# Values of nine tiles moved behind the routed loop, recurrence pieces inside the listing of rows, and gathered rows normalized on ScalarE

## The chip, the cores and the metric

The kernel runs on one core of a Trainium2 chip. A core has five engines that run side by side, each with its own in-order queue of instructions: PE (TensorE, matrix products and transposes), DVE (VectorE), ACT (ScalarE), POOL (GpSimd) and SP (SyncE, which here only issues DMA transfers). They meet through semaphores: an instruction waits until those it needs have signalled. The metric is the device time of one execution in microseconds (us), as the median of several runs; lower is better.

## The reference

There are 2048 tokens of 512 numbers in float32, and two layers. In each the input is normalized per row (`xn`), two branches are computed from `xn`, and `x = x + s * silu(ffn)`.

```python
xn = _layernorm(x)
# layer 0: s is a recurrence over the tokens, per channel
xk, xv, xr = (xn * tm + shifted(xn) * (1 - tm) for tm in (tm_k, tm_v, tm_r))
k, v, r = xk @ Wk.T, xv @ Wv.T, sigmoid(xr @ Wr.T)
def step((aa, bb, pp), (kt, vt)):
    qt = maximum(pp, kt + u); e1 = exp(pp - qt); e2 = exp(kt + u - qt)
    out = (e1 * aa + e2 * vt) / (e1 * bb + e2)
    pn = maximum(pp + neg_ew, kt); f1 = exp(pp - pn); f2 = exp(kt - pn)
    return (f1 * aa + f2 * vt, f1 * bb + f2, pn), out
s = (r * layernorm(out)) @ Wo.T
# layer 0: ffn is the better of 2 experts for each token (512 -> 2048 -> 512)
h = silu(x @ w_gate[e].T) * (x @ w_up[e].T);  y = (h @ w_down[e].T) * top_w
# layer 1: s is attention, keys before the last 256 of a batch averaged in blocks of 64
s = (softmax(mask(q @ k.T)) @ v) @ Wo
# layer 1: ffn is 2 shared experts and the best 4 of 16 routed ones (512 -> 352 -> 512)
rout = sum over the 4 chosen e of g[t, e] * (relu(x @ w1[e] + b1[e]) @ w2[e] + b2[e])
```

## The kernel before, in words

A tile is 128 tokens; there are 16. Python generators hand out pieces of one stage that are put between the matmuls of another, and a scheduler places each engine's instructions from there; `keep_in_program_order` pins an instruction to the place where it was written. PE carries the order of the whole: where it has nothing, other engines are late.

**First stage (lines 177 to 262).** Rows are loaded, normalized on ScalarE (L234), a difference of the two experts' logits `dl` is taken (L238), and each of the 16 tiles is transposed on PE (`transposed`, L139, with a copy on ScalarE, L140) and stored to `xnt0` in HBM (L245). After all 16 stores SP issues the loads of `wv` and `wr` (L248, L249). L250 copies the rows' means into `facts`.

**The listing (L252 to L361).** It lists the rows of each expert, so that tiles of 128 rows belong to one expert: `sel` (L253) on VectorE, sums with PE (`tab`, L271), a chain of small VectorE operations for the place of each row, then `put` (three operations, L343) and four `hot` matrices (L350), and 32 matmuls (L355) that bring row number, mean and `rstd` to their places. `tok` (L359) and `row_mr` (L360) are copies of the result. 17 tiles of listed rows come out, in pairs: nine steps of the expert loop, one of them a single tile.

**The recurrence (L386 to L536).** `recurrence(b)` handles a block of 256 tokens; 8 blocks of 22 pieces. A block loads `xT0` from `xnt0` (L393, L395), carries the last state over on ScalarE (L397), takes `diff` on GpSimd (L400), three mixes `xm` of four VectorE operations each (L406), projections on PE (L416) with copies of k and v on ScalarE (L428, L452), scans on VectorE (L435, L478), `f1`, `f2`, `qt` on VectorE (L459 to L463), `e1`, `e2` on GpSimd (L464, L465), two sigmoids and two Exps on ScalarE (L467 to L471), and the products, GpSimd taking `v` (L484), `den` (L492) and `r` (L534). Before the expert loop the generator is advanced by seven pieces (L692); the rest is spread over the loop.

**The expert loop of layer 0.** `rows0` gathers the listed rows on GpSimd's DMA queue (L545, four buffers `xr`), normalizes them on VectorE (L552), transposes them (`tp`, L560) and copies the result on ScalarE (`xg`, L563). `up0` makes `pg` on PE (L571, three PSUM buffers), `sg` on ScalarE (L576), `hT` on VectorE (L578). `down0` (L593) runs two steps behind. Each pair has 16 such steps. SP loads the weights in eight parts per pair (L157, L161), four buffers.

**The routed loop of layer 1 (L1715).** 80 tiles are laid out, of which those that hold rows run (later ones in a conditional). A tile has `tp` (L1661), `xg` (L1663), `ph` (L1668), `ht` (L943), `py` (L1692), `y` (L1697) and a scatter-add into `comb` on GpSimd's queue (L1700). Weights come on SP (L659 to L662). Pieces of the attention are put between the tiles: per block the queries and the scores, and for tiles 0 to 7 (`WIDE` is 8) the values. `PARTS` (L1706) is their number, 40. Tiles 0 to 7 have few pooled keys ("near", `vo8`), tiles 8 to 13 more ("wide", `vo`). `values` transposes the probabilities (`pt`, L1590), copies them on ScalarE (`sT`, L1595), multiplies with V and Wo already joined (`pw`, L1600) and copies to `xT` (L1604).

**The tail (L1737 to L1773).** Sums are loaded from `comb` (L1744) once all scatters have landed. `values` of tiles 8 to 11 follow, then `close(0)`, `close(2)`, `values(12)`, `close(4)`, `close(6)`, `values(13)` and the last four. A `close` handles two tiles: Silu on ScalarE (L1752, pinned), a product with `xT` (L1754) and a sum (L1758) on VectorE, and the store (L1759).

Of the kernel before, what the change touches and what calls it, by code (L numbers as in the profile page):

```python
# [17 lines left out]
P = 128  # L18
T = 2048
D = 512  # L20
# [57 lines left out]
def tile_kernel(ctx: ExitStack, tc: tile.TileContext, a: dict):  # L78
# [89 lines left out]


# [55 lines left out]
    for i in range(0, NT, 2):  # L225
        xin = xins[i // 2]
        mv, rstd = norm_stats(xin, 2, all_mv[:, i : i + 2, :], facts[:, 2, i : i + 2])
        shift = small.tile([P, 2], F32, tag="shift", name="shift")
# [3 lines left out]
        for j in range(2):  # L232
            xn = xin[:, j, :]
            nc.scalar.activation(  # L234
                xn, xn, AF.Identity, bias=shift[:, j : j + 1], scale=rstd[:, j : j + 1],
            )
            junk = n0.tile([P, D], F32, tag="hot", bufs=2, name="junk")
            nc.vector.tensor_tensor_reduce(  # L238
                out=junk, in0=xn, in1=wdiff, scale=1.0, scalar=0.0, op0=ALU.mult, op1=ALU.add,
                accum_out=dl[:, i + j : i + j + 1],  # L240
            )
    for i in range(NT):
        xt = n0.tile([P, NC, P], F32, tag="xt", name="xt")
        transposed(n0ps, xins[i // 2][:, i % 2, :], xt, "tp")
        nc.sync.dma_start(out=xnt0[:, :, i * P : (i + 1) * P], in_=xt)  # L245
    wv = rc.tile([P, NC, D], F32, name="wv")
    wr = rc.tile([P, NC, D], F32, name="wr")
    tc.keep_in_program_order(nc.sync.dma_start(out=wv, in_=a["Wv"]))  # L248
    tc.keep_in_program_order(nc.sync.dma_start(out=wr, in_=a["Wr"]))  # L249
    nc.vector.tensor_copy(facts[:, 1, :], all_mv[:, :, 0])  # L250

    sel = n0.tile([P, NT, E0], F32, bufs=1, name="sel")  # L252
    nc.vector.tensor_scalar(  # L253
        out=sel[:, :, 0], in0=dl, scalar1=0.0, scalar2=None, op0=ALU.is_le
    )
    nc.vector.tensor_scalar(
# [83 lines left out]

    put = n0.tile([P, NT, 3, NST], F32, bufs=1, name="put")
# [6 lines left out]
    for i0 in range(0, NT, HN):  # L348
        hot = n0.tile([P, HN, P], F32, tag="hot", bufs=2, name="hot")
# [20 lines left out]
    zero = rc.tile([P, DX], F32, name="zero")  # L370
    nc.gpsimd.memset(zero, 0.0)
    S4 = [P, NC, RB]
    ones = rc.tile([P, P], F32, name="ones")
    nc.vector.memset(ones, 1.0 / D)
    nge = rc.tile([P, NC], F32, name="nge")
    nc.scalar.activation(nge, vecs[:, VEC.index("decay"), :], AF.Exp)
    nc.vector.tensor_scalar(out=nge, in0=nge, scalar1=-1.0, scalar2=None, op0=ALU.mult)

    st_p = rc.tile([P, NC, RB + 1], F32, name="st_p")
    st_a = rc.tile([P, NC, RB + 1], F32, name="st_a")  # L380
    st_b = rc.tile([P, NC, RB + 1], F32, name="st_b")
    nc.vector.memset(st_p[:, :, 0:1], -1.0e38)
    nc.vector.memset(st_a[:, :, 0:1], 0.0)
    nc.vector.memset(st_b[:, :, 0:1], 0.0)

    def recurrence(b):  # L386

        t0 = b * RB

        xT0 = rb.tile([P, NC, RB + 1], F32, tag="xT0", bufs=2, name="xT0")  # L390
        if b == 0:
            nc.vector.memset(xT0[:, :, 0:1], 0.0)
            nc.sync.dma_start(out=xT0[:, :, 1:], in_=xnt0[:, :, 0:RB])  # L393
        else:
            nc.sync.dma_start(out=xT0, in_=xnt0[:, :, t0 - 1 : t0 + RB])  # L395
            for st in (st_p, st_a, st_b):
                nc.scalar.copy(st[:, :, 0:1], st[:, :, RB : RB + 1])  # L397
        cur, prev = xT0[:, :, 1 : 1 + RB], xT0[:, :, 0:RB]
        diff = rb.tile(S4, F32, tag="diff", name="diff")
        nc.gpsimd.tensor_tensor(out=diff, in0=cur, in1=prev, op=ALU.subtract)  # L400
        yield

        def mixed(tm):
            xm = rb.tile(S4, F32, tag="xm", bufs=3, name="xm")
            for c in range(NC):
                nc.vector.scalar_tensor_tensor(  # L406
                    out=xm[:, c, :], in0=diff[:, c, :], scalar=vec(tm, c),
                    in1=prev[:, c, :], op0=ALU.mult, op1=ALU.add,
                )
            return xm  # L410

        def project(xm, w_, o0):
            ps = rps.tile([P, 2, RB], F32, tag="proj", name="proj")
            for j in range(2):
                for c in range(NC):
                    nc.tensor.matmul(  # L416
                        out=ps[:, j, :], lhsT=w_[:, c, (o0 + j) * P : (o0 + j + 1) * P],
                        rhs=xm[:, c, :], start=(c == 0), stop=(c == NC - 1),
                    )
            return ps  # L420

        k = rb.tile(S4, F32, tag="k", name="k")
        ku = rb.tile(S4, F32, tag="ku", name="ku")
        v = rb.tile(S4, F32, tag="v", name="v")
        r = rb.tile(S4, F32, tag="r", name="r")

        def take_k(o0, ps):
            nc.scalar.copy(k[:, o0 : o0 + 2, :], ps)  # L428
            for j in range(2):
                nc.scalar.activation(  # L430
                    ku[:, o0 + j, :], ps[:, j, :], AF.Identity, bias=vec("first", o0 + j)
                )

        def scan_p(c):
            nc.vector.tensor_tensor_scan(  # L435
                out=st_p[:, c, 1 : RB + 1],
                data0=nge[:, c : c + 1].to_broadcast([P, RB]),
                data1=k[:, c, :], initial=st_p[:, c, 0:1], op0=ALU.add, op1=ALU.max,
            )

        xk = mixed("tm_k")
        yield
        xv = mixed("tm_v")
        take_k(0, project(xk, wk, 0))
        yield
        xr = mixed("tm_r")
        take_k(2, project(xk, wk, 2))
        yield
        for o0 in (0, 2):
            scan_p(o0)  # L450
            scan_p(o0 + 1)
            nc.scalar.copy(v[:, o0 : o0 + 2, :], project(xv, wv, o0))  # L452
            yield
        pp, ppn = st_p[:, :, 0:RB], st_p[:, :, 1 : RB + 1]
        ex = rb.tile([P, 4, NC, RB], F32, tag="ex", name="ex")
        e1, e2, f1, f2 = (ex[:, i] for i in range(4))
        qt = rb.tile(S4, F32, tag="qt", name="qt")
        r01 = project(xr, wr, 0)
        nc.vector.tensor_tensor(out=f1, in0=pp, in1=ppn, op=ALU.subtract)  # L459
        nc.vector.tensor_tensor(out=f2, in0=k, in1=ppn, op=ALU.subtract)  # L460
        yield
        r23 = project(xr, wr, 2)
        nc.vector.tensor_tensor(out=qt, in0=pp, in1=ku, op=ALU.max)  # L463
        nc.gpsimd.tensor_tensor(out=e1, in0=pp, in1=qt, op=ALU.subtract)  # L464
        nc.gpsimd.tensor_tensor(out=e2, in0=ku, in1=qt, op=ALU.subtract)  # L465
        yield
        nc.scalar.activation(r[:, 0:2, :], r01, AF.Sigmoid)  # L467
        nc.scalar.activation(r[:, 2:4, :], r23, AF.Sigmoid)
        yield
        nc.scalar.activation(ex[:, 2:4], ex[:, 2:4], AF.Exp)  # L470
        nc.scalar.activation(ex[:, 0:2], ex[:, 0:2], AF.Exp)  # L471
        fv = qt
        nc.vector.tensor_tensor(out=fv, in0=f2, in1=v, op=ALU.mult)
        yield

        def scan(st, add, cs):
            for c in cs:
                nc.vector.tensor_tensor_scan(  # L478
                    out=st[:, c, 1 : RB + 1], data0=f1[:, c, :], data1=add[:, c, :],
                    initial=st[:, c, 0:1], op0=ALU.mult, op1=ALU.add,  # L480
                )

        scan(st_a, fv, (0, 1))
        nc.gpsimd.tensor_tensor(out=v, in0=e2, in1=v, op=ALU.mult)  # L484
        yield
        scan(st_a, fv, (2, 3))
        yield
        scan(st_b, f2, range(NC))
        yield
        num, den = ku, fv  # L490
        nc.vector.tensor_tensor(out=num, in0=e1, in1=st_a[:, :, 0:RB], op=ALU.mult)
        nc.gpsimd.tensor_tensor(out=den, in0=e1, in1=st_b[:, :, 0:RB], op=ALU.mult)  # L492
        yield
        nc.vector.tensor_tensor(out=num, in0=num, in1=v, op=ALU.add)
        nc.vector.tensor_tensor(out=den, in0=den, in1=e2, op=ALU.add)
        yield
        for c0 in (0, 2):
            for c in (c0, c0 + 1):
                nc.vector.reciprocal(out=den[:, c, :], in_=den[:, c, :])
            yield  # L500


        two = rb.tile([P, 2, RB], F32, tag="two", name="two")

        def mean(src):

            nc.vector.tensor_tensor(out=two, in0=src[:, 0:2], in1=src[:, 2:4], op=ALU.add)
            nc.vector.tensor_tensor(
                out=two[:, 0, :], in0=two[:, 0, :], in1=two[:, 1, :], op=ALU.add
            )  # L510
            pm = f0t.tile([P, 2, RB], F32, tag="tp", name="pm")[:, 0, :]
# [1254 lines left out]
    for i in (0, 2):  # L1766
        close(i)
# [100 lines left out]
```

## Time and profile before

| | us |
|---|---|
| runs: lowest, median, highest of 3 | 1935.80, 1936.94, 1939.53 |
| the profiled execution | 1930.89 |
| its span on the core | 1929.2 |
| PE busy in the span | 1849.7 |
| mean granted PE clock | 0.984 of full |
| first expert matmul `pg` starts | 81.48 |
| last matmul of the routed loop ends | 1878.64 |
| first product of the tail on VectorE starts | 1900.49 |

The span runs from the first to the last instruction on the core; 1.69 us of the profiled execution lie around it. A row of a timeline gives the start, the busy time, the engine, the source line, the operation, the output and inputs with their shapes, how many instructions were joined, and in brackets the idle time before it on its engine with what ended it. PEld is PE's loading of weights; a letter q behind an engine's name means its queue of other instructions. A row of windows gives for a stretch the busy time and number of instructions of PE, PEld, DVE, ACT and POOL, then the granted clock, the busy share of the DMA engines and the GB/s. A row of waits gives who waited for whom: total, times, longest.

### The profile page before, as it was taken

What the parts mean: (1) busy time and instruction counts of PE and PEld (TensorE: products, weight loads), DVE (VectorE), ACT (ScalarE), POOL (GpSimd) and SP (SyncE); (2) the same over time, 40 slices, a digit from 0 to 9 for tenths busy, and PEclk for the clock granted to TensorE, in tenths of its full rate; (3) what the DMA queues carried; (4) which work ended last, traced back from release to release, by engine and by line L of the source; (5) the groups of instructions that cost most, each with busy time, mean ns of one, the idle gap of its engine ahead of it and who ended that gap; (6) DMA issues with size and microseconds to landing.
All of it is one profiled execution on the core that took longest, in us unless ns stands there. A gap on an engine that the chain in (4) does not pass through costs nothing. (4 is left out here: it accounts for less than half of the span.)

```text
span 1929.2 us, 23186 instructions
## 1 busy us (share of the span) xinstructions
PE 1849.7 (96%) x8107; PEld 1286.6 (67%) x8107; DVE 772.0 (40%) x1544; ACT 525.4 (27%) x989; POOL 467.0 (24%) x351
## 2 busy tenths in 40 slices
PE   5899999999999999999999999999999999999994
PEld 4677777787877777777533654445777777777662
DVE  8713637272634545252175543421323323233313
ACT  6213222232323232232134212221222222222222
POOL 1301212120201111020210453000344444444340
PEclk8899999999999999999999999999999999999997
DMA  7657685635654443536461553122999999999895
GB/s 252 208 156 265 222 304 180 216 106 165 197 192 142 132 131 124 160 97 229 155 227 48 177 206 115 50 82 83 316 291 311 325 283 277 276 269 269 232 254 183
DMA packets 214096, 381.35 MB, mean 198 GB/s; under 512 B 16972, under 2 KB 134476, under 8 KB 213080
## 3 DMA queue, kind: packets, MB, share of 16 engines
q1 hardware_dynamic: 183896, 332.78, 51.5%
q0 software_dynamic: 28784, 45.63, 10.8%
q10 hardware_dynamic: 1296, 1.41, 0.3%
q8 instruction: 67, 1.10, 0.2%
q14 instruction: 53, 0.43, 0.1%
HBM read 294.04 MB, written 85.72 MB: 197 GB/s over the span
## 5 line engine op out<-in xcount | busy, mean ns | idle before, releaser
L571 PE MATMUL pg<-xg,w 128*128 128x256 f32 (+1 forms) x2304 | 495.0, 367 | 3.6 <-ACT xg L563 3.6
L571 PEld LDWEIGHTS pg<-xg,w 128*128 128x128 f32 x2304 | 419.0, 190 | 94.4 <-issue 42.1
L1700 POOL DMA_INDIRECT comb<-y,to x146 | 227.5, 1558 | 317.6 <-DMA comb<-y,to 210.4
L593 PE MATMUL py<-wd,hT 128*128 128x512 f32 x544 | 256.9, 593 | 2.9 <-DVE hT L578 2.9
L1668 PEld LDWEIGHTS ph<-xg,w 128*128 128x128 f32 (+1 forms) x1776 | 201.9, 182 | 38.3 <-ACT xg L1663 33.3
L1668 PE MATMUL ph<-xg,w 128*128 128x128 f32 (+1 forms) x1776 | 214.5, 277 | 1.2 <-DMA w<-in_w_dram 1.2
L1692 PE MATMUL py<-w,ht 128*128 128x512 f32 (+1 forms) x438 | 207.8, 593 | 0.0
L578 DVE TENSOR_TENSOR hT<-sg,pg 128x256 f32<-128x256 f32 (+1 forms) x144 | 57.1, 402 | 335.7 <-ACT sg L576 335.6
L576 ACT ACTIVATE sg<-pg 128x256 f32<-128x256 f32 (+1 forms) x144 | 53.5, 372 | 416.9 <-PE pg L571 416.6
L593 PEld LDWEIGHTS py<-wd,hT 128*128 128x128 f32 x544 | 102.1, 190 | 72.2 <-issue 61.9
L1697 DVE TENSOR_SCALAR y<-py,g 128x512 f32<-128x512 f32 x73 | 54.6, 749 | 228.1 <-PE py L1692 228.1
L943 ACT ACTIVATE ht<-ph,b1t 128x128 f32<-128x128 f32 (+1 forms) x222 | 81.3, 366 | 178.5 <-PE ph L1668 178.0
L1692 PEld LDWEIGHTS py<-w,ht 128*128 128x128 f32 (+1 forms) x438 | 76.2, 191 | 53.3 <-issue 51.9
L1663 ACT COPY xg<-tp 128x512 f32<-128x512 f32 x74 | 43.4, 586 | 188.0 <-PE tp L1661 188.0
L1106 PE MATMUL py<-w,hT 128*128 128x512 f32 (+1 forms) x192 | 89.4, 595 | 0.0
L957 PE MATMUL ph<-xT,w 128*128 128x512 f32 (+1 forms) x192 | 88.0, 597 | 0.0
L1044 POOL DMA_INDIRECT xs<-acc,slot x64 | 64.0, 1000 | 65.9 <-DMA xs<-acc,slot 44.5
L416 PE MATMUL proj<-xm,wr 128*128 128x256 f32 x256 | 60.7, 392 | 5.8 <-ACT v L452 5.8
L712 PE MATMUL po<-wo,yb 128*128 128x512 f32 x128 | 58.9, 620 | 6.5 <-ACT acc L721 6.5
L464 POOL TENSOR_TENSOR ex<-st_p,qt 128x1024 f32<-128x1024 f32 x8 | 18.3, 2288 | 192.8 <-DVE qt L463 192.8
L1661 PEld LDWEIGHTS tp<-ident,x 128*128 128x128 f32 x296 | 36.7, 140 | 38.8 <-issue 20.8
L545 POOL DMA_INDIRECT xr<-in_x_dram,tok x17 | 23.2, 1365 | 160.4 <-PE tp L560 133.2
(412 smaller groups left out, 2182.7 us busy)
## 6 DMA issues: line engine op xcount, KB each, us to landing
w<-in_w_dram SPq DMA_DIRECT2D x76, 704.0 KB
w<-in_w_dram SPq DMA_DIRECT2D x76, 512.0 KB
w<-in_w_gate_dram SPq DMA_DIRECT2D x72, 512.0 KB
w<-in_w_up_dram SPq DMA_DIRECT2D x72, 512.0 KB
wd<-in_w_down_dram SPq DMA_DIRECT2D x72, 512.0 KB
xs<-zero SPq DMA_DIRECT2D x16, 1360.0 KB
x<-xs SPq DMA_DIRECT2D x74, 272.0 KB
w<-in_w_dram SPq DMA_DIRECT2D x76, 192.0 KB
```

The source lines that it names most:

```text
L416: nc.tensor.matmul(out=ps[:, j, :], lhsT=w_[:, c, (o0 + j) * P : (o0 + j + 1) * P], rhs=xm[:, c, :], start=(c == 0), stop=(c == NC - 1),)
L571: nc.tensor.matmul(out=pg[:, i, 0:n], lhsT=w[:, c, i * FH + f * P : i * FH + (f + 1) * P], rhs=xg[:, c, 0:n], start=(c == 0), stop=(c == N ...
L578: nc.vector.tensor_tensor(out=hT[:, 0:n], in0=sg[:, 0:n], in1=pg[:, 1, 0:n], op=ALU.mult)
L593: nc.tensor.matmul(out=p, lhsT=hT[:, u * P : (u + 1) * P], rhs=wd[:, f, :], start=first_, stop=last_,)
L712: nc.tensor.matmul(out=po, lhsT=yb[:, c, s * P : (s + 1) * P], rhs=wo[:, c, :], start=(c == 0), stop=(c == NC - 1),)
L943: nc.scalar.activation(dst, src, AF.Relu, bias=b)
L957: nc.tensor.matmul(out=ph[0:n, :], lhsT=up(w, f, n, c), rhs=xT[:, c, cols], start=(c == 0), stop=(c == NC - 1),)
L1044: ins = nc.gpsimd.indirect_dma_start(out=xs, out_offset=bass.IndirectOffsetOnAxis(ap=slot[:, i, k : k + 1], axis=0), in_=acc[:, i, :], in_ ...
L1106: nc.tensor.matmul(out=py, lhsT=hT[0:n, e, f, s * P : (s + 1) * P], rhs=down(w, f, n), start=(e == 0 and f == 0), stop=(e == NS - 1 and f ...
L1668: nc.tensor.matmul(out=ph[0:n, :], lhsT=up(w, f, n, c), rhs=xg[:, c, :], start=(c == 0), stop=(c == NC - 1),)
L1692: nc.tensor.matmul(out=py, lhsT=hT[0:n, f, :], rhs=down(w, f, n), start=(f == 0), stop=(f == NF1 - 1),)
L1700: nc.gpsimd.indirect_dma_start(out=c_, out_offset=bass.IndirectOffsetOnAxis(ap=to, axis=0), in_=y[:, h * D // 2 : (h + 1) * D // 2], in_of ...
```

## The change

1. `zero`, `ones`, `nge`, the states and `recurrence` are defined before the first stage. Two pieces are issued before `sel`, one before `put`, one before the third `hot`, and two more before the expert loop (six ahead of it; seven before). `diff` of blocks 0 and 1 goes to VectorE. Block 0's Exps, block 1's copies of the states and the first operation of `sel` are pinned.
2. `wv` and `wr` are loaded at tiles 4 and 8 of the transposes.
3. `shift` (minus mean times `rstd`) is written into `facts` in place of the mean, and gathered rows are normalized as `x * rstd + shift` on ScalarE.
4. `values` is cut in two: `turned` (transposes and the `sT` copy) and `values` (the matmuls and the `xT` copy). Tiles 5 to 13 (`LAST`) have theirs behind the routed loop, each tile's `turned` issued before the `values` of the tile ahead of it; `turned` of these takes PSUM from the pool of `py`. `PARTS` is 37. `close(0)` and `close(2)` follow the values of tile 11, 4 and 6 those of 12, 8 and 10 those of 13, then 14 and 12.

`recurrence` is the same code but for the lines shown.

```diff
+    zero = rc.tile([P, DX], F32, name="zero")
...
+    def recurrence(b):
...
             for st in (st_p, st_a, st_b):
-                nc.scalar.copy(st[:, :, 0:1], st[:, :, RB : RB + 1])
+                ins = nc.scalar.copy(st[:, :, 0:1], st[:, :, RB : RB + 1])
+                if b == 1:
+                    tc.keep_in_program_order(ins)
...
-        nc.gpsimd.tensor_tensor(out=diff, in0=cur, in1=prev, op=ALU.subtract)
+        (nc.vector if b < 2 else nc.gpsimd).tensor_tensor(
+            out=diff, in0=cur, in1=prev, op=ALU.subtract
+        )
...
-        nc.scalar.activation(ex[:, 2:4], ex[:, 2:4], AF.Exp)
-        nc.scalar.activation(ex[:, 0:2], ex[:, 0:2], AF.Exp)
+        ins = nc.scalar.activation(ex[:, 2:4], ex[:, 2:4], AF.Exp)
+        if b == 0:
+            tc.keep_in_program_order(ins)
+        ins = nc.scalar.activation(ex[:, 0:2], ex[:, 0:2], AF.Exp)
+        if b == 0:
+            tc.keep_in_program_order(ins)
...
-        shift = small.tile([P, 2], F32, tag="shift", name="shift")
+        shift = facts[:, 1, i : i + 2]
...
+    wv = rc.tile([P, NC, D], F32, name="wv")
+    wr = rc.tile([P, NC, D], F32, name="wr")
     for i in range(NT):
         xt = n0.tile([P, NC, P], F32, tag="xt", name="xt")
         transposed(n0ps, xins[i // 2][:, i % 2, :], xt, "tp")
         nc.sync.dma_start(out=xnt0[:, :, i * P : (i + 1) * P], in_=xt)
-    wv = rc.tile([P, NC, D], F32, name="wv")
-    wr = rc.tile([P, NC, D], F32, name="wr")
-    tc.keep_in_program_order(nc.sync.dma_start(out=wv, in_=a["Wv"]))
-    tc.keep_in_program_order(nc.sync.dma_start(out=wr, in_=a["Wr"]))
-    nc.vector.tensor_copy(facts[:, 1, :], all_mv[:, :, 0])
-
+        for at, w_, nm in ((4, wv, "Wv"), (8, wr, "Wr")):
+            if i == at:
+                tc.keep_in_program_order(nc.sync.dma_start(out=w_, in_=a[nm]))
+
+    blocks = (piece for b in range(NRB) for piece in recurrence(b))
+    for _ in range(2):
+        next(blocks)
...
+    tc.keep_in_program_order(ins)
...
+    next(blocks)
     put = n0.tile([P, NT, 3, NST], F32, bufs=1, name="put")
...
     for i0 in range(0, NT, HN):
+        if i0 == 2 * HN:
+            next(blocks)
         hot = n0.tile([P, HN, P], F32, tag="hot", bufs=2, name="hot")
...
-            nc.vector.tensor_scalar(
-                out=xr, in0=xr, scalar1=row_mr[:, 0, j : j + 1],
-                scalar2=row_mr[:, 1, j : j + 1], op0=ALU.subtract, op1=ALU.mult,
-            )
+            nc.scalar.activation(
+                xr, xr, AF.Identity, bias=row_mr[:, 0, j : j + 1], scale=row_mr[:, 1, j : j + 1]
+            )
...
-    for _ in range(7):
+    for _ in range(6 - done):
         next(blocks)
         done += 1
...
-    def values(i, s, pinned=False):
+    def turned(i):
+
+        s = waiting.pop(i)
         keys = s.shape[2]
         each = P // keys
-        by_row = vo if keys == KP else vo8
         nw = H // each
-        pt = aps.tile([P, nw, P], F32, tag="pa", name="pt")
+
+        pool, tag = (m1y, "py") if i in LAST else (aps, "pa")
+        pt = pool.tile([P, nw, P], F32, tag=tag, name="pt")
...
         sT = aq2.tile([P, HKV, P], F32, tag="sT", name="sT")
-        ins = nc.scalar.copy(sT[:, 0:nw, :], pt)
-        if pinned:
-            tc.keep_in_program_order(ins)
+        nc.scalar.copy(sT[:, 0:nw, :], pt)
+        return i, nw, sT, vo if keys == KP else vo8
+
+    def values(i, nw, sT, by_row):
...
+    LAST = range(5, FULL[0])
...
-                if i < WIDE:
-                    values(i, waiting.pop(i))
+                if i not in LAST:
+                    values(*turned(i))
                     yield
...
-    PARTS = 4 * nb + WIDE
+    PARTS = 4 * nb + LAST[0]
...
-    for i in (8, 9, 10, 11):
-        values(i, waiting.pop(i), pinned=True)
-    for i in (0, 2):
-        close(i)
-    values(12, waiting.pop(12), pinned=True)
-    for i in (4, 6):
-        close(i)
-    values(13, waiting.pop(13), pinned=True)
-    for i in (8, 10, 14, 12):
-        close(i)
+
+    pinned = tc.keep_in_program_order
+    closing = [i for i in range(0, NT, 2) if i < LAST[0] - 1]
+    closing += [i for i in (*range(0, NT, 2),) if i not in closing and i != FULL[0] - 2]
+    closing += [FULL[0] - 2]
+    ahead = turned(LAST[0])
+    for i in LAST:
+        now, ahead = ahead, turned(i + 1) if i + 1 in LAST else None
+        values(*now)
+        if i >= LAST[-1] - 2:
+            for _ in range(2):
+                close(closing.pop(0))
+    for i in closing:
+        close(i)
```

## The prediction

> **What bounds the kernel now.** I read the page's busy shares and slices first, then the timeline of the first 82 us and of the last 55, then the waits and the windows between.
>
> ```profile
> PE 1849.7 (96%) x8107; PEld 1286.6 (67%) x8107; DVE 772.0 (40%) x1544; ACT 525.4 (27%) x989; POOL 467.0 (24%) x351
> ...
> PE   5899999999999999999999999999999999999994
> ...
> PEclk8899999999999999999999999999999999999997
> ```
>
> TensorE works 96% of the span, at a lower clock only in the first two slices and the last. So only two things can move the end: matmul time taken off PE, and PE's holes, which sit at both ends. The windows and waits say it of the routed loop:
>
> ```profile
> 560.00:910.00 350.00, 350.00 (x1418) 267.00 (x1417) 148.25 (x184) 100.55 (x156) 47.05 (x21) 1.00 0.44 141
> 1400.00:1876.00 476.00, 475.30 (x2656) 344.39 (x2656) 136.50 (x442) 121.84 (x288) 203.01 (x132) 1.00 0.97 281
> ```
>
> ```profile
> SPq L660 <- PE py L1692: 196.3, 58, 7.2
> ```
>
> In the loop PE is busy 475.3 of 476 us, and the weight queue (L660) waits 196.3 us for PE's buffers: PE bounds it, though the DMA share is 0.97. The start, by its timeline:
>
> ```profile
> 37.22 2.33 POOL L400 TENSOR_TENSOR diff<-xT 128x1024 f32<-128x1024 f32 x1 [9.47 <-DVE run L279]
> ...
> 37.77 1.80 DVE L288 TENSOR_TENSOR full<-run,eno 128x8 f32<-128x8 f32 x1
> ...
> 46.54 7.07 PE L355 MATMUL tab<-put,hot 128*128 128x51 f32 x32 [5.31 <-DVE put L343]
> ...
> 53.64 0.18 DVE L359 CAST tok<-tab 128x17 int32<-128x17 f32 x1 [1.42 <-PE tab L355]
> ...
> 67.61 6.41 PE L416 MATMUL proj<-xm,wr 128*128 128x256 f32 x16 [5.77 <-ACT v L452]
> ...
> 81.48 0.70 PE L571 MATMUL pg<-xg,w 128*128 128x256 f32 x2 [3.56 <-ACT xg L563]
> ```
>
> Three holes of 5.31, 5.77 and 3.56 us. The first waits for the listing; the second for a ScalarE copy of v, queued behind an Exp that waits for GpSimd's e2 (62.79 to 65.14); the third for the copy of the gathered rows, queued behind state copies that wait for GpSimd. The first expert matmul starts at 81.48. The tail:
>
> ```profile
> 1881.22 0.63 PE L1590 MATMUL pt<-ident,wide 128*128 128x128 f32 x4 [2.91 <-PEq L1717]
> ...
> 1892.74 9.44 SPq L1744 DMA_DIRECT2D y<-comb  x16
> ...
> 1900.49 2.36 DVE L1754 TENSOR_TENSOR y<-xT,y 128x1024 f32<-128x1024 f32 x2 [24.18 <-DMA y<-comb]
> 1901.31 0.57 ACT L1595 COPY sT<-pt 128x512 f32<-128x512 f32 x1
> 1901.93 0.30 PEld L1600 LDWEIGHTS pw<-vo,sT 128*128 128x128 f32 x2 [4.26 <-ACT sT L1595]
> 1901.93 5.40 PE L1600 MATMUL pw<-vo,sT 128*128 128x512 f32 x8 [4.03 <-ACT sT L1595]
> ...
> 1908.94 2.36 DVE L1754 TENSOR_TENSOR y<-xT,y 128x1024 f32<-128x1024 f32 x2 [3.81 <-ACT y L1752]
> ```
>
> The loop's last matmul ends at 1878.64 (call it L). From 1900.49 VectorE sets the end: 16 operations at a pitch of 1.15 = 18.4 us, two holes (3.81, 2.12), then 4.33 us for the last store: the span's end is L+50.56.
>
> **The change, part by part.**
>
> *Tail.* Values of tiles 5, 6, 7 (1.79 us each: a loop tile's period is 7.61 with one, 5.82 without) and of tile 8 (1821.04 to 1825.85 with its pw, 4.81) leave the loop: 3 x 1.79 + 4.81 = 10.18 us of PE. In the tail PE now does 5 to 11 before the first Silu: 3 x 1.79 + 4 x 4.30 (0.60 + 3.70) = 22.6 (the 0.7 that each pw waited for its sT copy is covered by the next tile's transposes), plus 1.5 for the cold clock (pw took 5.20 after the 2.91 hole, 3.70 warm): from L+2.91 to L+27.0. Then the xT copy 0.59, the Silu's table load 1.28, half a pair of Silus 1.06: VectorE starts at L+29.9. The loads of comb (issued after a wait for the last scatter, landed L+19 before) are no longer last, and no longer on the path. Because tiles 12 and 13 are turned ahead, pw 12 ends by L+31.3 and pw 13 by L+35.1, Silus 4 and 6 by L+33.8: VectorE runs its 16 operations without a hole, 18.4, then 4.33: L+52.6. That is 2.0 later against L, with L 10.2 earlier: **-8.1**. Bounds: -9.6 if the clock stays up through the first hole, -6.5 if one more pair of VectorE operations waits (1.6).
>
> The trace has pw at 3.70 us after the hole of 2.61 (1910.38) and at 5.40 after 4.03. [...]
>
> *Start, listing.* VectorE gets more to do between sel (L253) and tok (L359): f1, f2 and qt of block 0 (L459 to L463, 1.13 pitch, 3.4 us; before they stood behind tok), diff of block 1 (1.22), and the last scans and mixes. GpSimd's e1 and e2 (2.19 + 2.35) then start right behind qt, near 47.4, and end near 51.9, in the middle of the listing, where VectorE's next operations are mixes with two SBUF inputs. An operation of 128x8 took 1.80 us beside GpSimd's diff (rows above), ending 0.02 after it; of a mix beside GpSimd no row exists. Between 0.48 (unhindered) and a wait to the end of e2 I take the latter, the nearest row: 4.2 us. So put ends near 55.1 (before 46.5: +3.4 +4.2 +1.0 for the other pieces, net of the 0.9 that sel is earlier), the tab matmuls take 7.07 plus two cold projections of 0.93, tok comes at 64.0, **10 us later than before**, and the gathers start at 65.1.
>
> [...]
>
> *Start, after the listing.* What waited behind the gathers is gone from the path: v copies stand ahead on ScalarE, e1 and e2 end before the gathers, both block-0 Exps stand after the first seven sg (L576). By the view of their line, gathers landed 3.3 to 7.6 us after issue (median 6.5), the slow ones under a DMA share of 1.02 at 346 GB/s (41 to 69 us). wv and wr are loaded earlier (at transposes 4 and 8; SP's loads of xnt0 and of FFN weights stand behind them, 4 weight buffers fill by about 62), so I take 4: 69. Normalization on ScalarE 0.75, tp 0.60, copy 0.58, the second tile's 0.75 + 0.60 + 0.58 and a sigmoid 0.60 between them; PE fills with 9 projections of wr until 70.5. First pg at 69 + 0.75 + 0.60 + 0.58 + 0.60 + 0.75 + 0.60 + 0.58 = 73.5, and I add 0.8 for queues: **74.3, or 7.2 earlier**. Bounds: 3.9 earlier if the landing takes 7.3, 11.4 if GpSimd blocks nothing. Besides, five projection matmuls more are done before the first pg: 5 x 0.464 = **-2.3**.
>
> *Normalization on ScalarE* (L552, 17 tiles). VectorE waited 42.4 us for gathers, 8.2 at most; now ScalarE's queue waits and the next sg stands behind. At 143.66 a gather was issued and landed by 151.33: 7.7, of which ScalarE would stand 5 to 6. The cover is three PSUM buffers of pg and down0 two steps behind, some two steps of 5.17 = 10 us; the first pair is nearest to it, as rows 5 and 6 (gathers after the first transposes) hold the first sg until about 83.5, with PE covered to 84.5. I take 0; bounds 0 to +2. Without that cover each of 8 pairs would cost 2 to 5.
>
> *The rest.* The copy of means (L250, 1.73 under GpSimd's diff) goes, and both diffs of 1.9 and 2.33 on GpSimd become 1.22 on VectorE; that makes sel 0.9 earlier and is in the walk. The pinned Exps wait for e2, done 25 us before they are reached; the pinned state copies stand among sg and wait for scans done by then; behind both is only sg, under the same cover of 10 us. On SP the loads of blocks 2 and 3 (L395) stand behind the first four weight sets, and the fifth set behind block 3's, which waits for VectorE's last mix of block 1: four steps, 20 us, cover it. Block 0's recurrence ends later, with PE at 350.00 of 350 us up to 910, so none of it is at the end. The loop's attention pieces go from 40 to 37 over the same 73 tiles: 0.
>
> **Sum**: -8.1 - 7.2 - 2.3 + 0 = -17.6. The profiled execution took 1930.89 (span 1929.2 and 1.69 around it), giving 1913.3; the median shown is 6.05 above it, so 1936.94 - 17.6 = **1919.3**. Bounds together: -11.4 - 2.3 - 9.6 = -23.3, and -3.9 - 2.3 - 6.5 + 2 = -10.7.
>
> **Rivals.** A. *The start gives nothing*: listing 10 later, landing slow, PE finds no work: first pg at 81.5 with the projections lost in the hole. For it: tok's delay is sure. Against: the removed waits (5.77 + 3.56 and cold clocks). Only the tail: 1936.94 - 8.1 = 1928.8.
>
> B. *The loop is set by DMA*: share 0.97, POOL waits 210.4 us for scatters. Then the loop keeps its length, the tail grows by 2.0: -9.5 + 2.0 = -7.5, 1929.4. Against: PE 475.3 of 476, and 346 GB/s moved elsewhere against 281.
>
> C. *ScalarE's queue behind late gathers*, the slower side. Place: sg behind the normalization in FFN. For it: rows that waited 8.2; single-tile steps are only 2.6 us (a hole of 2.9 at 529 to 546). It decides from a hold of about 10 us, and the sum turns slower once 8 pairs lose over 2.7 each (17.6 + 3.9 over 8); at 3 each, +6.4: 1943.
>
> D. *A and B together*: only the tail's 2.0 is left, 1938.9: within the bound of 0.2% (3.9 us, what can be told from no change).
>
> **How the numbers follow.** Forecast 0.60 (1919.3; 1913.6 to 1926.2), A 0.14, B 0.10, D 0.06, C 0.10. Faster 0.84, same 0.06, slower 0.10. The range goes from the lower bound, 1913, to just past A and B, 1931; outside are C, D and some of the forecast's ends.
>
> **What would show it.** Right: tok near 64, e1/e2 near 47 to 52 with a long VectorE row beside them, first pg near 74, the loop's last matmul 19.7 earlier (7.2 + 2.3 + 10.2), VectorE's last 16 operations without holes from about L+30. Wrong: first pg after 80; PE holes at 0.5 us and more ending in hT or sg during the FFN; loop periods unchanged where values left; y<-comb still the last wait of the tail.

## The result and the profile after

The changed kernel takes **1918.81 us** (median of 6 runs, 1917.98 to 1922.52) against 1936.38 us (median of 6, 1934.57 to 1939.53): ratio 0.9911, 95% interval 0.9898 to 0.9924, faster by 17.6 us. The profiled execution took 1917.98, its span is 1916.3. The forecast was 1919.3.

The page of the changed kernel: busy shares, PE and its clock in 40 slices.

```profile
PE 1846.6 (96%) x8107; PEld 1286.1 (67%) x8107; DVE 761.6 (40%) x1528; ACT 536.3 (28%) x1006; POOL 460.9 (24%) x349
...
PE   5999999999999999999999999999999999999996
...
PEclk9899999999999999999999999999999999999998
```

PE is still 96% busy; 3.1 us of its work are gone (1849.7 to 1846.6) and the span is 12.9 shorter, so most of the gain is holes. The windows inside the expert loop and the routed loop, and the weight queue's waits:

```profile
545.00:935.00 390.00, 389.96 (x1576) 296.80 (x1575) 148.98 (x189) 105.27 (x166) 47.04 (x21) 1.00 0.45 146
1385.00:1860.00 475.00, 474.82 (x2682) 346.15 (x2682) 139.35 (x457) 120.91 (x287) 201.71 (x130) 1.00 0.98 286
```

```profile
SPq L674 <- PE py L1710: 204.0, 59, 8.5
```

PE is busy 474.82 of 475 us in the routed loop and the weight queue still waits for PE's buffers, 204.0 us: taking 10 us of PE out has not made the DMA the bound, at a share of 0.98. The start, by its timeline:

```profile
48.18 2.17 POOL L267 TENSOR_TENSOR ex<-st_p,qt 128x1024 f32<-128x1024 f32 x1 [44.88 <-DVE qt L266]
48.35 2.28 DVE L209 SCALAR_TENSOR_TENSOR xm<-diff,vecs,xT 128x256 f32<-128x256 f32 x1
...
50.31 2.53 POOL L268 TENSOR_TENSOR ex<-ku,qt 128x1024 f32<-128x1024 f32 x1
...
50.56 2.32 DVE L512 TENSOR_SCALAR at<-at 128x16 f32<-128x16 f32 x1
...
55.41 3.66 PE L538 MATMUL tab<-put,hot 128*128 128x51 f32 x16 [3.00 <-DVE put L524]
...
64.22 0.18 DVE L542 CAST tok<-tab 128x17 int32<-128x17 f32 x1 [3.63 <-PE tab L538]
...
65.44 1.20 POOL L560 DMA_INDIRECT xr<-in_x_dram,tok  x1 [12.61 <-DMA w<-in_w_up_dram]
...
70.45 1.52 ACT L567 ACTIVATE xr<-xr,row_mr 128x512 f32<-128x512 f32 x2 [3.80 <-DMA xr<-in_x_dram,tok]
...
74.45 7.72 PE L585 MATMUL pg<-xg,w 128*128 128x256 f32 x35
...
81.12 0.82 ACT L590 ACTIVATE sg<-pg 128x256 f32<-128x256 f32 x2
```

e1 and e2 (L267, L268) stand in the listing. A mix (L209) takes 2.28 and a 128x16 operation (L512) 2.32, and they end 0.28 and 0.04 after GpSimd's. tok comes at 64.22, 10.6 later than before; the first rows have landed at 70.45, and the first pg starts at 74.45, 7.0 earlier. The tail:

```profile
1859.51 2.92 PE L1686 MATMUL ph<-xg,w 128*128 128x128 f32 x24
...
1866.80 0.69 PE L1606 MATMUL pt<-ident,near 128*128 128x128 f32 x4 [4.37 <-PEq L1735]
...
1882.36 9.89 SPq L1762 DMA_DIRECT2D y<-comb  x16
...
1890.74 0.58 ACT L1621 COPY xT<-pw 128x512 f32<-128x512 f32 x1 [2.79 <-PE pw L1617]
...
1891.34 1.28 ACT L1770 ACT_TABLE_LOAD   x1
...
1892.63 2.00 ACT L1770 ACTIVATE y<-y 128x1024 f32<-128x1024 f32 x2
...
1893.72 2.36 DVE L1772 TENSOR_TENSOR y<-xT,y 128x1024 f32<-128x1024 f32 x2 [33.29 <-ACT y L1770]
...
1895.16 3.70 PE L1617 MATMUL pw<-vo,sT 128*128 128x512 f32 x8 [0.59 <-ACT sT L1611]
...
1909.62 2.36 DVE L1776 TENSOR_TENSOR y<-y,xo 128x1024 f32<-128x1024 f32 x2
```

The loop's last matmul ends at 1859.51 + 2.92 = 1862.43 (L; before, by the same rows, 1878.31: the 1878.64 given further up is 0.33 too late, which moves no difference here). VectorE starts at L+31.3, 1.1 us after the first Silu starts, and runs to the end without a hole. The span ends at L+53.9. ScalarE goes from the xT copy of tile 11 to the table load and the Silu without a hole, so VectorE's start is set by PE's matmuls and these operations, not by the sums from comb. (The other six executions of this tail show the same on ScalarE, though the profile puts VectorE's wait there down to y<-comb: the label names the signal that came last by the profile.) The row of the kernel before with "24.18 <-DMA y<-comb" has to be read in the same way, for there, too, ScalarE had no hole:

```profile
1897.51 0.59 ACT L1604 COPY xT<-pw 128x512 f32<-128x512 f32 x1 [3.79 <-PE pw L1600]
1898.11 1.28 ACT L1752 ACT_TABLE_LOAD   x1
1899.40 2.00 ACT L1752 ACTIVATE y<-y 128x1024 f32<-128x1024 f32 x2
```

Only in its second profile (before_again) did ScalarE wait for the sums, 0.96 us ahead of the table load and 0.44 ahead of the second Silu.

Stage by stage, in us, for every execution with a profile in this study. "to routed" runs from the last pg to the routed loop's first transpose, "loop" from there to the last ph, "tail" from there to the end; "records" are the projection matmuls before the first pg.

| execution | first pg | records | expert loop | to routed | loop | tail | span |
|---|---|---|---|---|---|---|---|
| before | 81.48 | 94 | 861.9 | 399.8 | 535.1 | 50.8 | 1929.2 |
| before_again | 80.59 | 94 | 863.4 | 401.6 | 534.0 | 52.3 | 1931.9 |
| after | 74.45 | 104 | 860.7 | 399.3 | 528.1 | 53.8 | 1916.3 |
| after_again | 74.93 | 104 | 861.2 | 402.7 | 524.3 | 54.4 | 1917.6 |
| start_alone | 73.48 | 104 | 861.4 | 401.9 | 535.5 | 56.4 | 1928.8 |
| tail_alone | 83.94 | 94 | 865.0 | 402.1 | 526.4 | 54.0 | 1931.4 |
| norm_on_vector | 75.12 | 102 | 861.1 | 401.1 | 524.7 | 53.8 | 1915.7 |
| e1_e2_on_vector | 73.42 | 114 | 858.3 | 403.0 | 528.8 | 55.8 | 1919.3 |
| wv_wr_late | 74.41 | 72 | 869.0 | 404.0 | 524.7 | 53.3 | 1925.3 |
| closes_earlier | 74.50 | 104 | 861.2 | 403.1 | 526.2 | 51.5 | 1916.5 |
| values_5_to_7_in_loop | 74.12 | 104 | 861.1 | 403.1 | 530.0 | 48.7 | 1917.1 |
| both_8 | 75.54 | 114 | 858.7 | 403.8 | 530.5 | 52.8 | 1921.2 |
| both_7_earlier | 73.88 | 114 | 859.0 | 402.2 | 527.7 | 51.1 | 1913.8 |
| rows_before_weights | 70.45 | 114 | 858.8 | 401.7 | 524.0 | 54.2 | 1909.2 |

The stretch "to routed", which no kernel here changes, lies between 399.3 and 404.0: a single profile is good to some 2 us there, and the same in the loop, where the first tile may wait for its weights (below). The old start puts its first pg at 80.6 to 83.9 in three executions.

### The profile page after: what moved, and what is told of

The parts are those of the page before. It is cut to its first block, busy times and chain, and to the rows that moved or that the text cites. A ratio compares the mean times of both kernels' runs of the same rounds, so it can differ in the third digit from the quotient of the medians.

```text
span 1916.3 us, 23192 instructions
## 1 busy us (share of the span) xinstructions
PE 1846.6 (96%) x8107; PEld 1286.1 (67%) x8107; DVE 761.6 (40%) x1528; ACT 536.3 (28%) x1006; POOL 460.9 (24%) x349
## 3 DMA queue, kind: packets, MB, share of 16 engines
q10 hardware_dynamic: 1296, 1.41, 0.2%
## 5 line engine op out<-in xcount | busy, mean ns | idle before, releaser
L267 POOL TENSOR_TENSOR ex<-st_p,qt 128x1024 f32<-128x1024 f32 x8 | 18.3, 2287 | 236.1 <-DVE qt L266 236.1
L219 PE MATMUL proj<-xm,wk 128*128 128x256 f32 x256 | 59.0, 383 | 0.0
```

The costliest lines, as they stand in the source:

```text
L219: nc.tensor.matmul(out=ps[:, j, :], lhsT=w_[:, c, (o0 + j) * P : (o0 + j + 1) * P], rhs=xm[:, c, :], start=(c == 0), stop=(c == NC - 1),)
```

## The experiments

Ratios are to runs of the kernel before on the same chip.

**The two parts by themselves.** `start_alone` is the changed kernel without the hunks on `values`, `LAST`, `PARTS` and the closes; `tail_alone` is the kernel before with these alone.

> The changed kernel with the tail's part undone: recurrence pieces in the listing, early loads of wv and wr, normalization on ScalarE, and the tail as before. My theory: -7.2 for the first expert matmul and -2.3 for projections already done, -9.5 us, ratio near 0.9951; first pg at 74.3. Rival (the gain at the start is lost again later in the expert loop, since ScalarE is held by gathers): ratio 0.998 or more with the first pg still at 74. If the two parts are independent, the two ratios' distances from 1 add up to 0.0089.

> The kernel before with the tail's part alone (values of tiles 5 to 13 behind the routed loop, the next tile turned ahead, new order of the closes). My theory: -8.1 us, a ratio near 0.9958; the routed loop about 9.8 shorter between its first and last matmul, VectorE's last 16 operations without a hole. Rival (the DMA or the scatters set the loop): the loop keeps its length and the run is 0 to 2 us slower, ratio 1.000 to 1.001. Rival (the tail gives nothing, all came from the start): ratio 1.000.

Measured: start_alone 0.9961 (0.9944 to 0.9977), first pg at 73.48; tail_alone 0.9941 (0.9922 to 0.9960), the loop at 526.4 against 534.0 and 535.1. The distances from 1 add up to 0.0098 against 0.0089 for both, as two independent gains would within these intervals: about 8 us for the start and 11 for the tail by the ratios, 7.6 and 9.0 by the medians of the same runs. The rivals in which one part or the loop gives nothing are out. The size of the tail's gain is less sure: in the trace of tail_alone, loop and tail together take 580.4 against 585.9 and 586.3, 5.5 to 5.9 less. The tail of start_alone is the old one, and shows by its timeline what its holes can cost:

```profile
1876.95 0.73 PE L1603 MATMUL pt<-ident,wide 128*128 128x128 f32 x4 [4.60 <-PEq L1730]
...
1878.36 6.57 PE L1613 MATMUL pw<-vo,sT 128*128 128x512 f32 x8 [0.68 <-ACT sT L1608]
...
1899.13 6.42 PE L1613 MATMUL pw<-vo,sT 128*128 128x512 f32 x8 [4.03 <-ACT sT L1608]
...
1908.60 5.11 PE L1613 MATMUL pw<-vo,sT 128*128 128x512 f32 x8 [2.62 <-ACT sT L1608]
```

pw takes 6.57, 6.42 and 5.11 here, after holes of 0.68 (behind one of 4.60), 4.03 and 2.62; in the first profile of before it took 5.20, 5.40 and 3.70, with the last two holes the same (4.03, 2.61). The granted clock over these three pw was 0.71, 0.68 and 1.00 there; by their lengths against the 3.70 at 1.00 it is about 0.56, 0.58 and 0.72 here, an estimate. The old tail thus took 50.8, 52.3 and 56.4 in three executions. Of the 5.6 between the first and the last, 1.7 are the hole behind the loop (4.60 for 2.91) and 3.8 the longer pw (1.37, 1.02 and 1.41); the 52.3 holds the 1.4 us that ScalarE waited for the sums. The new tail has a single long hole and took 53.3 to 55.8 in the seven executions that have it unaltered.

**The normalization's place.**

```diff
-            nc.scalar.activation(
-                xr, xr, AF.Identity, bias=row_mr[:, 0, j : j + 1], scale=row_mr[:, 1, j : j + 1]
-            )
+            nc.vector.tensor_scalar(
+                out=xr, in0=xr, scalar1=row_mr[:, 1, j : j + 1],
+                scalar2=row_mr[:, 0, j : j + 1], op0=ALU.mult, op1=ALU.add,
+            )
```

> The changed kernel with the gathered rows normalized on VectorE again (multiply and add, same order of everything else as far as the scheduler keeps it). My theory: the normalization's place costs or gains nothing in the expert loop, so the ratio to the kernel before stays at 0.991 within 0.001. Rival A (ScalarE held by gathers costs up to 2 us in the changed kernel): 0.990. Rival B (the move is what made the start short, because VectorE is full of mixes there and its rows would be late): first pg later than 76 and a ratio of 0.992 to 0.994.

Measured: 0.9898 (0.9873 to 0.9922), first pg at 75.12, the expert loop 861.1 against 860.7 and 861.2. The ratio by itself does not part the theory (0.991) from rival A (0.990); the expert loop does, as the 2 us of rival A are not in it. No difference: this part of the change costs and gains nothing that can be seen, though ScalarE waits 50.9 us for gathers in the changed kernel, 9.1 at most.

**What GpSimd's e1 and e2 cost the listing.**

```diff
-        nc.gpsimd.tensor_tensor(out=e1, in0=pp, in1=qt, op=ALU.subtract)
-        nc.gpsimd.tensor_tensor(out=e2, in0=ku, in1=qt, op=ALU.subtract)
+        eng = nc.vector if b == 0 else nc.gpsimd
+        eng.tensor_tensor(out=e1, in0=pp, in1=qt, op=ALU.subtract)
+        eng.tensor_tensor(out=e2, in0=ku, in1=qt, op=ALU.subtract)
```

> The changed kernel with e1 and e2 of block 0 on VectorE. If GpSimd's e1 and e2 block VectorE in the listing (mixes of 2.28 and a tensor_scalar of 2.32 in the changed kernel's timeline in place of 0.48 and 0.17, 3.95 us), the block is gone and two operations at 1.13 are added: tok 1.7 us earlier, 62.5 in place of 64.2, and the first pg by 0.8 to 1.7. Rival (the long rows of VectorE had another cause): the long rows stay and tok is 2.3 us later, 66.5.

Its timeline, the same operations as above:

```profile
48.51 1.22 DVE L268 TENSOR_TENSOR ex<-st_p,qt 128x1024 f32<-128x1024 f32 x1
...
49.64 0.17 DVE L513 TENSOR_SCALAR at<-at 128x16 f32<-128x16 f32 x1
...
53.55 0.48 DVE L209 SCALAR_TENSOR_TENSOR xm<-diff,vecs,xT 128x256 f32<-128x256 f32 x1
53.70 0.99 PE L539 MATMUL tab<-put,hot 128*128 128x51 f32 x8
...
58.70 0.18 DVE L543 CAST tok<-tab 128x17 int32<-128x17 f32 x1 [0.77 <-PE tab L539]
...
59.92 1.21 POOL L561 DMA_INDIRECT xr<-in_x_dram,tok  x1 [56.62 <-DMA w<-in_w_gate_dram]
...
67.26 0.81 ACT L568 ACTIVATE xr<-xr,row_mr 128x512 f32<-128x512 f32 x1 [5.30 <-DMA xr<-in_x_dram,tok]
...
73.42 10.60 PE L586 MATMUL pg<-xg,w 128*128 128x256 f32 x48
```

The 128x16 operation takes 0.17 and the mix 0.48: the long rows were GpSimd's doing, 1.80 + 2.15 = 3.95 us. tok is 5.5 earlier: the tab matmuls start 1.7 earlier, as expected, and the rest is PE's clock (from 41 to 69 us 0.94 granted, where the changed kernel's first profile has 0.76). PE has no hole of 3.00 before them and does eight in 0.99, 0.12 each, where that profile has sixteen in 3.66, 0.23 each, at a granted clock of 0.50. But the gathers, issued at 59.92, land at 67.26, 7.3 later, and the first pg gains only 1.0. Ten more records are done by then, and the expert loop is 2.4 shorter. Ratio 0.9875 (0.9846 to 0.9904).

The second profile of the changed kernel says the same without an edit:

> The changed kernel, unchanged, for a second profile and a ratio beside the two candidates on one chip. Ratio to the kernel before 0.989 to 0.993; first pg at 74 to 75.5; from the loop's last matmul to the end 53 to 54.5 us; the routed loop 525 to 528.

Ratio 0.9901 (0.9878 to 0.9925). Its first sixteen tab matmuls took 1.88 in place of 3.66:

```profile
57.11 1.88 PE L538 MATMUL tab<-put,hot 128*128 128x51 f32 x16
...
61.68 0.18 DVE L542 CAST tok<-tab 128x17 int32<-128x17 f32 x1 [1.17 <-PE tab L538]
...
62.90 1.21 POOL L560 DMA_INDIRECT xr<-in_x_dram,tok  x1 [9.46 <-DMA wd<-in_w_down_dram]
...
69.66 0.81 ACT L567 ACTIVATE xr<-xr,row_mr 128x512 f32<-128x512 f32 x1 [6.46 <-DMA xr<-in_x_dram,tok]
```

tok is 2.5 earlier than in the first profile and the first pg 0.5 later: rows issued at 62.90 landed at 69.66, 6.8 later, where those issued at 65.44 had taken 5.0.

**Holding back the weights.** On top of e1_e2_on_vector the third and fourth set of expert weights wait for the second gather.

```diff
-                w, wd, came = load0(e, part)
+                w, wd, came = load0(e, part, gathered[1] if at_ == 0 and 1 < part < 4 else None)
...
+            if behind is not None:
+                tc.add_manual_dep(ins.ins, behind, AFTER, reason="rows go first")
```

> e1 and e2 of block 0 on VectorE (as in e1_e2_on_vector), and the third and fourth set of expert weights wait until the second gather has landed. In five executions tok came between 58.7 and 64.2 and the first gathered rows landed between 67.0 and 70.5, 5.0 to 7.3 us after issue, the first pg between 73.4 and 75.1. Theory: the weight loads under way stretch the gathers, so an earlier listing buys little; with the loads held back the rows land 3.3 to 4 us after issue, at 63.2 to 64, and the first pg comes 6.2 later as in e1_e2_on_vector, at 69.5 to 70.5, 3 us earlier than there. Rival (a gather's landing after the listing is set by something else than the weight loads): landing again 7 us after issue, first pg at 73 to 75.

Timelines and one window (56 to 70 us: busy times, then clock, DMA share and GB/s), first of this kernel and then the window of e1_e2_on_vector:

```profile
59.34 0.18 DVE L545 CAST tok<-tab 128x17 int32<-128x17 f32 x1 [0.77 <-PE tab L541]
...
60.55 1.20 POOL L565 DMA_INDIRECT xr<-in_x_dram,tok  x1 [57.26 <-DMA xT<-xnt]
...
64.42 0.81 ACT L573 ACTIVATE xr<-xr,row_mr 128x512 f32<-128x512 f32 x1 [1.84 <-DMA xr<-in_x_dram,tok]
...
70.45 10.63 PE L591 MATMUL pg<-xg,w 128*128 128x256 f32 x48 [0.43 <-ACT xg L583]
```

```profile
56.00:70.00 14.00, 11.14 (x64) 9.23 (x63) 4.70 (x13) 4.85 (x8) 7.26 (x7) 1.00 0.72 227
```

```profile
56.00:70.00 14.00, 8.93 (x48) 7.78 (x47) 4.66 (x12) 2.22 (x3) 4.33 (x4) 0.85 1.06 374
```

With the DMA at 0.72 in place of 1.06 the rows land 3.9 us after issue and pg starts at 70.45, 3.0 earlier: with this listing, the weight loads under way hold back the first pg (one execution of each). The span is the shortest of the study, 1909.2, but the runs (median 1916.15, ratio 0.9890, 0.9866 to 0.9913) don't set it apart from the change.

**Early loads of wv and wr.** Both are issued after the last transpose again.

```diff
-        for at, w_, nm in ((4, wv, "Wv"), (8, wr, "Wr")):
-            if i == at:
-                tc.keep_in_program_order(nc.sync.dma_start(out=w_, in_=a[nm]))
+    for w_, nm in ((wv, "Wv"), (wr, "Wr")):
+        tc.keep_in_program_order(nc.sync.dma_start(out=w_, in_=a[nm]))
```

> The changed kernel with wv and wr loaded after all 16 transposes, as before the change. My theory (the early loads feed projections that fill PE while the listing is made): the projections of v slide behind the listing, the holes of PE before the first pg add up to 3 to 8 us more and the first pg comes at 77 to 82 in place of 74.4. Rival (the early loads matter little, since PE has time while it waits for the listing): first pg within 1 us of 74.4.

```profile
42.96 0.62 SPq L425 DMA_DIRECT2D wv<-in_Wv_dram  x1
...
50.21 1.19 PE L219 MATMUL proj<-xm,wv 128*128 128x256 f32 x2 [10.04 <-DMA wv<-in_Wv_dram]
...
59.10 0.18 DVE L541 CAST tok<-tab 128x17 int32<-128x17 f32 x1 [2.75 <-PE tab L537]
...
74.41 5.80 PE L584 MATMUL pg<-xg,w 128*128 128x256 f32 x20
```

PE stands 10.04 us for wv, as the theory said, but the first pg is at 74.41, as the rival said: the projections slide behind pg. 72 records are done by then in place of 104, and the expert loop is 8 us longer (869.0): 32 records at 0.232 (178.0 us for 768 in the changed kernel) are 7.4. Ratio 0.9928 (0.9901 to 0.9954); after_again has 0.9901 on another chip, 5 us less, with intervals that overlap. In the same comparison as wv_wr_late, with a median of 1924.9, three other variants of the change have 1914.9 to 1918.4. The early loads are worth the 8 us of the expert loop in the traces, and the first pg doesn't show it. That is all that the start gains: without them the expert loop ends at 943.4, where the kernel before has 943.3 and 944.0 (948.9 in tail_alone) and the changed kernel 935.1 and 936.1. An earlier first pg without them is worth 0 to 5.6 us in these profiles. Whether the early loads would be enough by themselves, without the pieces in the listing, was not run.

**The tail's order.** The first edit is `closes_earlier`, the second `values_5_to_7_in_loop` (the closes stay in their order).

```diff
-        if i >= LAST[-1] - 2:
+        if i >= LAST[-1] - 3:
```

```diff
-    LAST = range(5, FULL[0])
+    LAST = range(8, FULL[0])
```

> The changed kernel with each pair of closes one tile earlier (0 and 2 follow the values of tile 10 in place of 11, and so on). What bounds the tail of the changed kernel after its loop's last matmul (L) is the place of the first Silu behind the xT copy of tile 11, by my theory: VectorE then starts at about L+27.4 in place of L+31.3 and the last store ends at L+50 in place of L+53.8; against the changed kernel -3.9 us. Rival (the sums from comb land last, at L+24.6 at the earliest, and pw of tile 12 now waits behind the Silus with a cold clock): the start moves by less than 1 us or the operations of VectorE get holes, and the end stays within 1.5 us of L+53.8.

> The changed kernel with the values of tiles 5, 6, 7 back in the routed loop and those of 8 to 13 behind it. By my theory moving these three to the tail gains next to nothing, since PE sets the tail's start as well: the loop is 5.0 us longer (3 x 1.65) and the tail 5 to 6 shorter, VectorE starting at L+25 when the sums land: within 1.5 us of the changed kernel. Rival (the tail has slack for these three, its start is set by the sums or the Silus): the tail keeps 53.8 and the run is 5 us slower than the changed kernel.

closes_earlier: ratio 0.9895 (0.9859 to 0.9931); VectorE starts at L+29.0, 2.3 earlier and not 3.9, still without holes, and the tail is 2.3 shorter, between the theory and the rival. The Silu does stand one tile earlier; PE reached that tile 1.6 later after L than in the first profile (a hole of 4.87 in place of 4.37, and behind it a pt of 1.09 and pw of 3.78 and 2.21 in place of 0.69, 3.44 and 1.88). values_5_to_7_in_loop: 0.9892 (0.9864 to 0.9921); the tail is 5.1 shorter, the loop 2 to 6 longer: moving these three gains nothing by itself, as expected. Here the sums land just when ScalarE needs them: the first Silu stands right behind its table load, the second waits 0.27 us, by its timeline:

```profile
1888.38 9.63 SPq L1762 DMA_DIRECT2D y<-comb  x16
...
1893.27 1.06 ACT L1770 ACTIVATE y<-y 128x1024 f32<-128x1024 f32 x1
...
1894.36 2.55 DVE L1772 TENSOR_TENSOR y<-xT,y 128x1024 f32<-128x1024 f32 x2 [28.01 <-DMA y<-comb]
1894.59 1.06 ACT L1770 ACTIVATE y<-y 128x1024 f32<-128x1024 f32 x1 [0.27 <-DMA y<-comb]
```

**Two candidates that join these.** Both have e1 and e2 of block 0 on VectorE and keep the order of the closes. In this order, they have the edits

```diff
-    LAST = range(5, FULL[0])
+    LAST = range(8, FULL[0])
```

```diff
-    LAST = range(5, FULL[0])
+    LAST = range(7, FULL[0])
...
-        if i >= LAST[-1] - 2:
+        if i >= LAST[-1] - 3:
```

> e1 and e2 of block 0 on VectorE, and the values of tiles 5 to 7 back in the loop (8 to 13 behind it). If the effects add: against the changed kernel -2 to -3 up to the end of the expert loop (first pg 1.0 earlier, ten matmul records more done before it, 2.3 us) and 0 from the loop and tail: ratio 0.988 to 0.990, tail 48 to 50. Rival (what the start gains is noise of the gathers): the same ratio as the changed kernel.

> e1 and e2 of block 0 on VectorE, the values of tiles 7 to 13 behind the loop, and each pair of closes one tile earlier. The sums from comb land near L+25 and set VectorE's start (L+26): the loop 3.3 longer than the changed kernel's, the tail 5 shorter, so 1.7 better there, and 2 to 3 at the start: ratio 0.987 to 0.989, tail near 49. Rival (ScalarE, standing before the first Silu until the sums land, holds the sT copy of tile 12 and VectorE gets holes): tail 51 or more.

both_8: 0.9907 (0.9883 to 0.9932), tail 52.8 and not 48 to 50: ScalarE waited 3.62 us for the sums ahead of the first Silu, the sT copy of tile 12 stood behind it, and PE's hole there was 5.14. This is the mechanism that the rival named for both_7_earlier. both_7_earlier: 0.9888 (0.9862 to 0.9914), with the same hole at 4.48 and a tail of 51.1 and not 49, as its rival said. Against after_again's 0.9901 in the same comparison neither is told apart. No version here is shown to beat the change.

**The kernel before once more.**

> The kernel before, unchanged, to see what a second profiled execution of it looks like and how far two sets of runs of one kernel lie apart. The first profiled execution took 1930.89 against a median of 1936.4. If that one was a lucky draw, this profile's span is near 1934 to 1936 and the 5 us lie in waits for transfers between the expert loop and the routed loop (the first expert matmul again at 81.5, the tail again 50.5 long); if executions with a profile are shorter as such, it is near 1929 again. Ratio 1.000 within 0.001.

Ratio 0.9995 (0.9979 to 1.0010); its profiled execution took 1933.59 against a median of 1937.89 over 12 runs from 1932.29 to 1943.96. Neither case came out clean, since 4 us of the first profile's 6 under the median are there again. An execution with a profile is not shorter as such: in tail_alone, e1_e2_on_vector and wv_wr_late it was the slowest of its six runs, in rows_before_weights the fastest.

## Why the prediction held

*Tail, -8.1.* Two terms were mis-sized, both to the same side. The loop's own saving was put at 10.18; from the second tile's transpose to the last it is 9.77. But the first tile's weights came later in the first profile of the change, which left 7.1 (first the row before, then after); the second pair of profiles has 9.7:

```profile
1348.10 2.90 PE L1668 MATMUL ph<-xg,w 128*128 128x128 f32 x24 [1.21 <-DMA w<-in_w_dram]
```

```profile
1340.34 4.34 PE L1686 MATMUL ph<-xg,w 128*128 128x128 f32 x24 [2.25 <-DMA w<-in_b_dram]
```

The tail was to grow by 2.0 and grew by 3.0 and 2.1, since the hole behind the loop, taken over at 2.91, is 4.37 and 4.65; it is 3.7 to 5.0 in all kernels but the one before, and why stays open. Loop and tail together give about -4 and -7.6 in the two pairs of profiles, in place of -8.1, and the loop's last matmul came 15.9 and 16.4 earlier, not 19.7. VectorE did run without a hole. The sums are not on the path now, but in the profile that the prediction read they had not been last either, whatever the label said. That they land later now was not foreseen: their loads are issued at L+19.9, not L+14.4.

*Listing, 10 later.* tok 64.0 forecast, 64.22 measured; the block 4.2 and 3.95. The step was right, and its choice by the nearest row too. The half clock of the tab matmuls, taken for certain, was there in one of two executions (sixteen in 3.66 at 0.50 in the first, in 1.88 in the second).

*First pg, 74.3.* 74.45 and 74.93. The sum was right, but not for all its reasons: the landing took 5.0 where 4 was taken, and the 0.8 for queues stands in for it. What the prediction had wrong is that each microsecond of the listing is one of the first pg. The ten executions that have the new start and hold back no weights have tok from 58.5 to 64.4 and the first pg between 73.4 and 75.5, in no order with it.

*Projections, -2.3.* Ten records more are done before pg, as forecast; the expert loop is 1.2 shorter in the first pair, 2.2 in the second.

*Normalization, 0.* Held: the first sg starts at 81.12, before the forecast's 83.5, and PE has no hole over 0.5 there. Holes that end in hT, which the prediction named as a sign of being wrong, are found only at the single-tile step, 0.97, 1.23 and 0.91 us from 521 to 538; the kernel before has them too (0.96, 1.24 and 0.70).

*Rivals.* A (the start gives nothing) and B (the loop keeps its length) are out by start_alone and tail_alone, and D (both together) with them; C (ScalarE's queue, slower) by norm_on_vector.

*The sum.* The medians differ by 17.6 as forecast, the two pairs of profiles, in which the terms can be seen, only by 12.9 and 14.3. The old tail, with three holes, varies by 5.6 and the first profile has its shortest form; that explains a part. The rest of the gap between profiled and other runs of the kernel before is not settled, so the exact hit of the forecast is in part luck.

## What to carry to other kernels

Work that waits in front of a full machine is worth moving into the holes ahead of it even when the chain it joins becomes longer: the listing grew by 10 us, and taking 5.5 of them back brought the first pg only 1.0 earlier, since the next wait, a gather among weight loads, was set elsewhere. Look past the first event for the gain: late weights left the first expert matmul where it was and cost 8 us behind it, as much as the whole start had gained. In a tail, work moved out of a loop that PE bounds gained nothing by the move, for three tiles of nine. What gains is, by these traces, that a copy stands ahead of the long operations in its queue, so that the next matmul finds its input: PE's holes of 4.03 and 2.61 are down to one of 0.59, and VectorE's of 3.81 and 2.12 are gone. No run has this order without any move.

## What the runs showed of the hardware

An operation of 128x16 with one tensor input on VectorE took 2.32 us beside a GpSimd subtraction and 0.17 without it, and a mix 2.28 and 0.48 (after, e1_e2_on_vector); why a GpSimd operation lengthens them was not shown. Gathers of 128 rows took 3.9 us to land at a DMA share of 0.72 and 7.3 at 1.06 (rows_before_weights, e1_e2_on_vector).

Holes of 2.6 us on PE were followed by a pw of 3.70 in two executions (before, where the granted clock over it was 1.00, and before_again) and of 5.11 in another (start_alone). So one and the same hole was followed by a slower pw or not; what decides it was not shown.
